# A graph attention layer on one core: SyncE fetches the rows of one gathered tile in every 22nd pair

## The chip, the cores and the metric

The kernel runs on one core of a Trainium2 chip. A core has five engines with a queue of instructions each: TensorE (PE), VectorE (DVE), ScalarE (ACT), GpSimd (POOL) and SyncE (SP). DMAs are issued from a queue of an engine and run on 16 DMA engines. The metric is the device time in microseconds, the median of the runs.

## The reference, cut to what matters

One layer of graph attention (GATv2) with layer norms and a feed forward part, on 12,500 nodes of 128 features and 400,000 edges. The edges are sorted by destination. All is in float32.

```python
h = relu(layernorm(x))
hn = ln1(h)
x_l, x_r = hn @ W_l, hn @ W_r                      # [nodes, 8 heads, 16]
m = leaky_relu(x_l[src] + x_r[dst] + ea @ W_e, 0.2)  # per edge
alpha = einsum("ehc,hc->eh", m, att)
a = softmax of alpha over the edges of one destination (and a self loop)
o = segment_sum(x_l[src] * a, dst) + bias
h = h + o
out = x + h + gelu(ln2(h) @ W1 + b1) @ W2 + b2
```

What matters here is `x_l[src]`: for each edge one row of 136 numbers (544 B: the 128 of x_l and eight ones for the sum of weights) is fetched from `xl_dram` by the index of the source. These are 3125 tiles of 128 edges.

## The kernel before, in words

**Units.** A unit is 256 edges (two tiles of 128), a pair is two units (512 edges, four tiles), and four pairs share one window of nodes. There are 782 pairs. The nodes are in 98 tiles of 128.

**The start.** A first stage reads x and writes the rows of x_l to `xl_dram` (`x_l`, L595 and L603, four tiles of nodes at a time). It also loads the edges' sources (`src_sb`, L797, one column per tile), the first destinations (`first_sb`, `base_sb`, L266) and makes the tables from which SyncE later reads addresses (`win_sb`, `base_sb`). Meanwhile GpSimd gathers raw rows of x for 29 pairs (`raw`, L301), stores them (`raw_dram`), and their x_l is worked out later from these (`late_dram`), so that these 29 pairs need no gather from `xl_dram`.

**The rounds.** The rest (`window_edges`) is one long list written out by hand, a loop over rounds `r`. Each engine has its instructions in the order of this list. In round `r` the steps of the list are applied to pair `c = r - late`, where `late` stands in a table:

- `gather` (-4): GpSimd issues four indirect DMAs, one for each tile of the pair, into `xs` (L980). Twelve buffers.
- `windows` (-3, once in four pairs): SyncE issues the loads of the edges' features `ea` (L994, two buffers, each freed by `combine` of its last pair), of the destinations `dl` and `du` (L999, L1004), reads one address from `win_sb` (L955) and loads the window of x_r, `zw` (L1010).
- `place` (-1): DVE makes the one-hot matrices. `combine` (0): PE transposes the rows of `xs` (L1034) and adds the window's product (L1037).
- `slope`, `bend`, `apart`, `score`, `lowest`, `weigh`, `turn`, `keep_turned` (1 to 5): the scores and their exponentials.
- `collect` (6): PE sums the weighted rows of `xs` (L1097). It is the last reader of `xs`.
- `own_heads` (7): DVE picks the heads and writes the records of the pair, `rec` (L1106, L1112).
- `put` (7): SyncE stores the record to `state` at an address read from `base_sb` (L1122, L955). Windows of 16 nodes of neighbouring units overlap, so stores are in order.

Between these stand the steps of node groups (four tiles of nodes, once all edges of the group are stored): loads of x_l, x_r and x, of the states (`f_state`, L1173), the end of the softmax and the feed forward part, and the store of the output (L1423). A group's round is found from the last unit that can touch its nodes (`done_after`). Further steps work out x_r (`xr_steps`) and the rows of the 29 late pairs (`raw_steps`), and in the first 196 rounds sum the edges' features (`ea_s`, L1129).

**Clearing.** `state` has two halves, for even and odd units. `clear` (L745) writes an empty value to seven tiles of nodes, a DMA for each half, once before the rounds and then every eighth round.

A DMA that touches bytes that an earlier one touches waits for it on the issuing engine: clearings, stores and the groups' loads of `state` have addresses from registers, so each is ordered behind the others.

Of the kernel before, what the change touches and what calls it, by code (L numbers as in the profile page):

```python
# [22 lines left out]
P = 128  # L23
H = 8
# [18 lines left out]
OW = 172  # L43
OS = 176
PW = OR * OS
BEFORE = 12
AFTER = 3
WN = P - DE
# [6 lines left out]
NQ = 16  # L55
SPARE = 8
AHEAD = 4
WAHEAD = 3
XR_STEPS = 6
RAW_MORE = 6  # L60
RAW_SHIFT = 8
# [1 line left out]
BUSY = 5  # L63
LEAD = 2
KEPT = 7
BIG = 2.0**126
CAP = 2.0**120

# [59 lines left out]
def raw_pairs(nt, n_edges):  # L128

    n_pr = -(-n_edges // (UP * U))  # L130
    at = [xr_round(t, nt, n_edges) + XR_STEPS + 1 for t in range(GN, nt, GN)]
    at = at[:-1] + [r + RAW_SHIFT for r in at[:RAW_MORE]]
    return [(r + RAW_STEPS + AHEAD + 1, r) for r in at if r + RAW_STEPS + AHEAD + 2 < n_pr]


def heads_of(nc, pool, out, att_c, fh):
# [8 lines left out]
def tile_gnn(  # L145
# [54 lines left out]

    h_sb = keep.tile([P, NT, P], F32, name="h_sb")
    src_sb = keep.tile([P, NCH * K], I32, name="src_sb")
    base_sb = keep.tile([1, NU // UP], I32, name="base_sb")
    win_sb = keep.tile([1, NU // QU], I32, name="win_sb")
# [49 lines left out]
    def load_consts():  # L254
        for i, v in enumerate((ln2_g, ln2_b, None, b1[0:P], b1[P : 2 * P])):
            if v is not None:
                nc.sync.dma_start(cols[:, 2 + i : 3 + i], column(v))
        nc.sync.dma_start(att_c, bass.AP(tensor=att.tensor, offset=att.offset, ap=[[1, C], [C, H], [1, 1]]))
        nc.sync.dma_start(we_sb, bass.AP(tensor=w_e.tensor, offset=w_e.offset, ap=[[P, DE], [0, QP], [1, P]]))
        nc.sync.dma_start(weh_sb[WN:P, :], w_e)  # L260
        nc.sync.dma_start(w1_sb, w1)
        nc.sync.dma_start(w2_sb, w2.rearrange("(k p) f -> p k f", p=P))
        nc.sync.dma_start(bias_r, row_bcast(bias, P))
        nc.sync.dma_start(b2_r, row_bcast(b2, P))
        for t, at in ((first_sb, 0), (base_sb, U)):
            nc.sync.dma_start(t, bass.AP(tensor=dst.tensor, offset=dst.offset + at, ap=[[0, 1], [UP * U, NU // UP]]))  # L266
# [103 lines left out]
    def edge_constants():  # L370
        of = build.tile([P, H], F32, name="of")
        mine = build.tile([P, H], F32, name="mine")
        below = build.tile([P, P // NW], F32, name="below")
        nc.vector.tensor_scalar(win_sb, first_sb[:, 0 : NU // UP : QP], float(P * 4), None, op0=OP.mult)
        nc.vector.tensor_scalar(first_sb, first_sb, float(BEFORE), None, op0=OP.add)
        nc.vector.tensor_tensor(base_sb, base_sb, first_sb, op=OP.min)
        nc.vector.tensor_scalar(base_sb, base_sb, float(H * SH * 4), None, op0=OP.mult)
# [362 lines left out]

    empty = keep.tile([P, H, SH], F32, name="empty")

    def clear(g):
        for st in state:
            nc.sync.dma_start(  # L745
                st.rearrange("(t p h) f -> p t (h f)", p=P, h=H)[:, g * GT : (g + 1) * GT, :],
                empty.rearrange("p h f -> p (h f)")[:, None, :].to_broadcast([P, GT, SW]),
            )

    node_stages = (  # L750
        (0, x_stats),
# [16 lines left out]
    with tc.manual_schedule():  # L768
# [15 lines left out]
        for r in range(max(max(len(qs), 9) + LAST + 1, 16 + PARTS, rows_at[-1] + KEPT + 1)):  # L784
# [10 lines left out]
                last_of_units()  # L795
            if r == 14:
                nc.sync.dma_start(src_sb, src)  # L797
            if r == 10:
                from_first()
            if 0 <= r - 10 < PARTS:  # L800
# [21 lines left out]
        clear(0)  # L822
    pre.close()

    fast = nc.values_load(flag[0:1, 0:1], min_val=0, max_val=1)
    with tc.If(fast == 1) as cmp:
        window_edges(
            tc, n_edges, ea_t, NT, NE, NUE, ident, wer, weh, negrep, diag, nid, farw, bias_r, b2_r, w1_sb, w2_sb,
            cols, xl_dram, xl_t, xr_dram, xr_t, dc_dram, du_dram, late_dram, state_dram, state, clear, xr_steps, qs, raw_steps, raw, x_t, out_t, h_sb, src_sb, base_sb, win_sb, wid,
        )  # L830
    with cmp.Else():
        any_edges(
# [64 lines left out]

def window_edges(
    tc, n_edges, ea_t, NT, NE, NUE, ident, wer, weh, negrep, diag, nid, farw, bias_r, b2_r, w1_sb, w2_sb,
    cols, xl_dram, xl_t, xr_dram, xr_t, dc_dram, du_dram, late_dram, state_dram, state, clear, xr_steps, qs, raw_steps, raw, x_t, out_t, h_sb, src_sb, base_sb, win_sb, wid,  # L900
):


# [25 lines left out]
    with ExitStack() as es:  # L929
# [34 lines left out]
        def states_at(at):  # L964
# [4 lines left out]
                "u (n f) -> n u f", f=SH * 4  # L969
            )  # L970

        def gather(c):
            xs = rows.tile([P, KP, XW], F32, name="xs")
            if c in of_raw:
# [2 lines left out]
                return  # L977
            for t in tiles_of(c):
                for j in t:
                    nc.gpsimd.indirect_dma_start(  # L980
                        out=xs[:, j, :],
                        out_offset=None,
                        in_=xl_dram,
                        in_offset=bass.IndirectOffsetOnAxis(ap=src_sb[:, c * KP + j : c * KP + j + 1], axis=0),
                    )
            pairs[c]["xs"] = xs

        def windows(c):
            if c % QP:
# [19 lines left out]
            at = words(win_sb[0:1, c // QP : c // QP + 1], NT * P * P * 4)[0]  # L1009
            nc.sync.dma_start(zw[0:WN, :].bitcast(U8), rows_at(xr_dram, at, WN, P * 4))  # L1010
# [18 lines left out]
        def combine(c):  # L1029
# [2 lines left out]
            z = ps2.tile([P, EPR], F32, name="z")  # L1032
            for j in range(e // P):
                nc.tensor.matmul(  # L1034
                    z[:, j * P : (j + 1) * P], d["xs"][:, j, 0:P], ident, start=(j == 0), stop=False, is_transpose=True
                )
            nc.tensor.matmul(z[:, :e], d["zw"], d["ea"][:, :e], start=False, stop=True)  # L1037
            d["z"] = z
# [51 lines left out]
        def collect(c):  # L1090
# [4 lines left out]
            for i, js in enumerate(tiles_of(c)):  # L1095
                for j in js:
                    nc.tensor.matmul(  # L1097
                        d["acc"][:, i, :], d["pt"][:, j * P : (j + 1) * P], d["xs"][:, j, :],
                        start=(j == js[0]), stop=(j == js[-1]),
                    )  # L1100

# [13 lines left out]

        def put(c):
            if c % QP == 0:
                at = words(base_sb[0:1, c : c + QP], NT * P * H * SH * 4)
                for i in range(c, min(c + QP, n_pr)):
                    pairs[i]["put"] = at[i - c]  # L1120
            d, nu = pairs[c], len(tiles_of(c))
            nc.sync.dma_start(states_at(d["put"])[:, 0:nu], d["rec"][:, 0:nu].bitcast(U8))  # L1122


        sums = [None] * NL
# [43 lines left out]
        def f_state(d):  # L1169
            n, ts = d["n"], d["ts"]  # L1170
            d["st"] = own_tile(d, "st", lambda n: [P, 2, n, SW], F32, "big", 3)
            for i in range(2):
                nc.sync.dma_start(d["st"][:, i, 0:n], state[i].rearrange("(t p h) f -> p t (h f)", p=P, h=H)[:, ts, :])  # L1173

        def f_load(d):
            n, ts = d["n"], d["ts"]
# [245 lines left out]
        def f_put(d):  # L1422
# [114 lines left out]
        last_round = n_pr + LATE + 2  # L1537
        free = SUM_STEP * (NL - 1) + 7
        for d, u in zip(groups, done_after(NT, n_edges)):
            d["round"] = max(free, (u // UP if u < NUE else n_pr) + LATE + 2)  # L1540
            free = d["round"] + GAP
        end["round"] = n_pr + LATE + 2

# [14 lines left out]
        CLEAR = 8  # L1558
        with tc.manual_schedule():
            for r in range(-AHEAD, max(last_round, groups[-1]["round"] + 18)):  # L1560
                in_round(r, early, groups[:-2])
# [15 lines left out]
                in_round(r, last_steps, groups[-1:])  # L1577
                in_round(r, enumerate(xr_steps), qs[1:])
                in_round(r, enumerate(raw_steps), raw)
                for late, f in late_stages:  # L1580
                    c = r - late
                    if 0 <= c < n_pr:
# [355 lines left out]
```

## Time and profile before

| | |
|---|---|
| median of 3 runs | 3962.19 us |
| the runs | 3970.01, 3962.19, 3960.23 us |
| the profiled execution | 3956.45 us |
| its span (first to last instruction) | 3954.7 us |
| busy share PE, DVE, ACT, POOL | 87%, 71%, 55%, 75% |
| granted TensorE clock, mean | 0.943 |
| DMA | 552.09 MB, mean 140 GB/s |

A group of instructions in the profile is a line of the program, an engine and an operation, what it writes and reads, the count, the busy time and the mean of one in ns, and behind the bar the idle time of the engine just before them with what ended it. "issue" is time in which the engine waited for nothing that the profile shows. SPq is SyncE's queue; its issuing instructions are not counted as busy, but each has a start and a length. Times of a timeline are start and length in us, from the start of the span.

### The profile page before, as it was taken

What the parts mean: (1) busy time and instruction counts of PE and PEld (TensorE: products, weight loads), DVE (VectorE), ACT (ScalarE), POOL (GpSimd) and SP (SyncE); (2) the same over time, 40 slices, a digit from 0 to 9 for tenths busy, and PEclk for the clock granted to TensorE, in tenths of its full rate; (3) what the DMA queues carried; (4) which work ended last, traced back from release to release, by engine and by line L of the source; (5) the groups of instructions that cost most, each with busy time, mean ns of one, the idle gap of its engine ahead of it and who ended that gap; (6) DMA issues with size and microseconds to landing.
All of it is one profiled execution on the core that took longest, in us unless ns stands there. A gap on an engine that the chain in (4) does not pass through costs nothing. (4 is left out here: it accounts for less than half of the span.)

```text
span 3954.7 us, 58500 instructions
## 1 busy us (share of the span) xinstructions
PE 3447.8 (87%) x18462; PEld 2358.8 (60%) x18463; DVE 2792.9 (71%) x6137; ACT 2168.7 (55%) x4747; POOL 2956.0 (75%) x3138
## 2 busy tenths in 40 slices
PE   4589898989898899999898898998889899889898
PEld 3356565656565666666665665666666566556565
DVE  6577777878776767677767776777767667667665
ACT  7445555655565555555555555555555555455444
POOL 7777777777777777777777777777777777777774
PEclk6799999999999999999999999999999999999999
DMA  8777787777666666666566666556556665655553
GB/s 225 214 183 190 195 201 194 184 176 168 164 128 124 128 122 123 128 123 120 115 122 128 124 123 128 123 119 125 117 124 125 127 122 108 122 119 114 122 118 74
DMA packets 579318, 552.09 MB, mean 140 GB/s; under 512 B 286689, under 2 KB 457282, under 8 KB 578578
## 3 DMA queue, kind: packets, MB, share of 16 engines
q1 hardware_dynamic: 478280, 330.80, 35.9%
q0 software_dynamic: 100000, 217.32, 28.5%
q8 instruction: 150, 2.46, 0.3%
q14 instruction: 168, 1.38, 0.1%
q10 hardware_dynamic: 720, 0.13, 0.0%
HBM read 482.05 MB, written 65.88 MB: 139 GB/s over the span
## 5 line engine op out<-in xcount | busy, mean ns | idle before, releaser
L980 POOL DMA_INDIRECT xs<-xl_dram,src_sb x3009 | 2841.7, 944 | 917.1 <-issue 798.0
L1075 ACT ACTIVATE p<-ab,rec 128x256 f32<-128x256 f32 x1563 | 655.2, 471 | 1025.8 <-DVE rec L1064 1021.3
L1106 DVE TENSOR_TENSOR own<-acc,diag 128x272 f32<-128x272 f32 x782 | 341.4, 437 | 811.5 <-PE acc L1097 809.5
L1097 PE MATMUL acc<-xs,pt 128*128 128x136 f32 x6250 | 891.6, 288 | 0.3 <-DVE own L1106 0.3
L1034 PE MATMUL z<-ident,xs 128*128 128x128 f32 x3125 | 552.9, 283 | 374.0 <-DMA xs<-xl_dram,src_sb 324.9
L1037 PE MATMUL z<-ea,zw 128*128 128x512 f32 x1564 | 852.7, 628 | 26.5 <-DVE ea L1020 11.3
L1034 PEld LDWEIGHTS z<-ident,xs 128*128 128x128 f32 x3125 | 398.4, 143 | 768.4 <-DMA xs<-xl_dram,src_sb 413.6
L1097 PEld LDWEIGHTS acc<-xs,pt 128*128 128x128 f32 x6250 | 820.7, 199 | 0.5 <-DVE own L1106 0.5
L1058 PE MATMUL ab<-m,negrep 128*128 128x512 f32 x1564 | 806.4, 597 | 0.0
L1088 ACT COPY pt<-pt_ps 128x512 f32<-128x512 f32 x782 | 454.9, 582 | 570.9 <-PE pt_ps L1083 568.9
L1053 DVE TENSOR_TENSOR m<-z,zs 128x512 f32<-128x512 f32 x782 | 532.8, 681 | 139.2 <-ACT zs L1048 138.1
L1083 PEld LDWEIGHTS pt_ps<-ident,p 128*128 128x128 f32 x3125 | 415.9, 148 | 360.1 <-issue 286.4
L1020 DVE TENSOR_SCALAR ea<-dl,wid 96x516 f32<-96x516 bf16 x782 | 575.8, 736 | 36.1 <-DMA dl<-dc_dram 36.1
L1064 DVE TENSOR_REDUCE rec<-ab 128x2 f32<-128x512 f32 x781 | 538.0, 689 | 13.1 <-PE ab L1058 12.5
L1083 PE MATMUL pt_ps<-ident,p 128*128 128x128 f32 x3125 | 499.4, 285 | 1.2 <-ACT xr L627 0.9
L1048 ACT ACTIVATE zs<-z 128x512 f32<-128x512 f32 x782 | 472.7, 604 | 41.7 <-DMA xs<-xl_dram,src_sb 34.9
L1112 DVE TENSOR_REDUCE rec<-own 128x34 f32<-128x272 f32 x782 | 340.8, 436 | 26.7
L1043 PE MATMUL ab<-ne,farw 128*128 128x512 bf16 x782 | 313.0, 400 | 28.4 <-ACT p L1075 25.7
L1037 PEld LDWEIGHTS z<-ea,zw 128*128 128x128 f32 x1564 | 256.5, 205 | 30.1 <-DVE ne L1027 10.3
L1058 PEld LDWEIGHTS ab<-m,negrep 128*128 128x128 f32 x1564 | 245.1, 194 | 1.1 <-DMA ea_s<-in_ea_t 0.7
L1043 PEld LDWEIGHTS <-farw 128*128 128x128 bf16 x782 | 79.5, 102 | 221.9 <-issue 110.2
L1075 ACT ACT_TABLE_LOAD x104 | 133.4, 1283 | 1.8
(237 smaller groups left out, 2167.4 us busy)
## 6 DMA issues: line engine op xcount, KB each, us to landing
dl<-dc_dram SPq DMA_DIRECT2D x196, 396.0 KB
ea<-in_ea_t SPq DMA_DIRECT2D x196, 256.0 KB
ea_s<-in_ea_t SPq DMA_DIRECT2D x98, 512.0 KB
xs<-xl_dram,src_sb POOLq DMA_INDIRECT x3009
state<-empty SPq DMA_DIRECT2D x28, 504.0 KB
state<-rec SPq DMA_DIRECT2D x781, 18.0 KB
f_st<-state SPq DMA_DIRECT2D x46, 288.0 KB
du<-du_dram SPq DMA_DIRECT2D x196, 64.0 KB
```

Source lines behind the costliest of these rows:

```text
L980: nc.gpsimd.indirect_dma_start(out=xs[:, j, :], out_offset=None, in_=xl_dram, in_offset=bass.IndirectOffsetOnAxis(ap=src_sb[:, c * KP + j ...
L1020: nc.vector.tensor_scalar(d["ea"][0:WN].rearrange("p (a b) -> p a b", b=OW), d["dl"][0:WN].rearrange("p (a b) -> p a b", b=OS)[:, :, 0:OW] ...
L1034: nc.tensor.matmul(z[:, j * P : (j + 1) * P], d["xs"][:, j, 0:P], ident, start=(j == 0), stop=False, is_transpose=True)
L1037: nc.tensor.matmul(z[:, :e], d["zw"], d["ea"][:, :e], start=False, stop=True)
L1048: nc.scalar.activation(d["zs"][:, :e], d["z"][:, :e], AF.Copy, scale=SLOPE)
L1053: nc.vector.tensor_tensor(d["m"][:, :e], d["z"][:, :e], d["zs"][:, :e], op=OP.max)
L1058: nc.tensor.matmul(d["ab"][:, :e], negrep.rearrange("p n h -> p (n h)"), d["m"][:, :e], start=False, stop=True)
L1064: nc.vector.tensor_reduce(d["rec"][:, :, CX], d["ab"].rearrange("p (u e) -> p u e", e=U), AX.X, OP.min)
L1075: nc.scalar.activation(d["p"][:, us], d["ab"][:, us], AF.Exp, bias=d["rec"][:, i, CX:SH], scale=-1.0)
L1083: nc.tensor.transpose(d["pt_ps"][:, js], d["p"][:, js], ident)
L1088: nc.scalar.copy(d["pt"][:, :e], d["pt_ps"][:, :e])
L1097: nc.tensor.matmul(d["acc"][:, i, :], d["pt"][:, j * P : (j + 1) * P], d["xs"][:, j, :], start=(j == js[0]), stop=(j == js[-1]),)
```

## The change

- Every 22nd pair from 30 to 778 (35 pairs, `hand_pairs`) gets only three gathers from GpSimd. The rows of its last tile are fetched by SyncE: 128 DMAs of one row each, at an address that SyncE reads from a table `hand_sb` (16 at a time), into one of two tiles of their own. They are spread over 22 rounds that end two rounds before the pair's use (`hand`). Each counts up one of seven semaphores, and SyncE waits for the full count in the round before the pair's use; PE's use is ordered behind this wait.
- `hand_sb` (35 partitions of 128 indices) is loaded at the start right behind `src_sb`, by one DMA of single words, and multiplied by the length of a row on DVE two rounds later.
- The addresses of windows and stores stand in one table `at_sb`, five words for four pairs, read at once. It is loaded by four DMAs in place of one.
- Loads of `windows` are issued four rounds ahead (`WAHEAD`, 3 before), and `put` stands one round later (`LATE + PUT`, 8 in place of 7). The node groups' rounds move with it, and `done_after` counts 12 nodes more.
- `clear` writes one tile of nodes for both halves in one DMA, four tiles before the rounds and then one every fourth round. A clearing isn't ordered behind stores so far, and a store isn't ordered behind loads of node groups before it. Stores stay ordered among themselves.

```diff
-WAHEAD = 3
+WAHEAD = 4
+PUT = 2
+BEHIND = 3
+HAND_EVERY = 22
+HAND_FIRST = 30
+HAND_LEAD = 2
+HAND_READ = 16
+LANDED = 7
...
-    return [-(-(t + n) * P * edges_per_node(nt, n_edges) // U) + SPARE for t, n in node_groups(nt)]
+    return [-(-((t + n) * P + BEFORE) * edges_per_node(nt, n_edges) // U) + SPARE for t, n in node_groups(nt)]
...
+        for i in range(QP):
+            nc.sync.dma_start(
+                at_sb[:, BEHIND:, 1 + i],
+                bass.AP(tensor=dst.tensor, offset=dst.offset + (UP * i + 1) * U, ap=[[0, 1], [QU * U, NQU]]),
+            )
...
             if r == 14:
                 nc.sync.dma_start(src_sb, src)
+                nc.sync.dma_start(
+                    hand_sb,
+                    bass.AP(
+                        tensor=src.tensor, offset=src.offset + (hands[0] + 1) * UP * KU - 1,
+                        ap=[[hands.step * UP * KU, len(hands)], [NCH * K, P]],
+                    ),
+                )
+            if r == 16:
+                nc.vector.tensor_scalar(hand_sb, hand_sb, float(XW * 4), None, op0=OP.mult)
...
+        def hand(r):
+
+            i, k = divmod(r + HAND_LEAD + hands.step - hands[0], hands.step)
+            if k == HAND_LEAD - 1 and 0 < i <= len(hands):
+                all_here = nc.sync.wait_ge(landed[(i - 1) % LANDED], ((i - 1) // LANDED + 1) * P * 16)
+                tc.declare_fence(all_here.ins, group=f"hand{i - 1}")
+            if not 0 <= i < len(hands):
+                return
+            d = by_hand[hands[i]]
+            if k == 0:
+                d["x"] = once.tile([P, XW], F32, name=f"hand{i % 2}")
+            for e in range(P * k // hands.step, P * (k + 1) // hands.step):
+                if e % HAND_READ == 0:
+                    d["at"] = words(hand_sb[i : i + 1, e : min(e + HAND_READ, P)], (NT * P - 1) * XW * 4)
+                row = nc.sync.dma_start(
+                    d["x"][e : e + 1, :].bitcast(U8), rows_at(xl_dram, d["at"][e % HAND_READ], 1, XW * 4)
+                )
+                row.then_inc(landed[i % LANDED], 16)
+                tc.no_tile_sem_insts.add(row.ins.name)
+                tc.add_to_no_dep_group(f"hand{i}", row.ins)
...
             for t in tiles_of(c):
                 for j in t:
+                    if c in by_hand and j == KP - 1:
+                        continue
                     nc.gpsimd.indirect_dma_start(
...
-            nc.sync.dma_start(states_at(d["put"])[:, 0:nu], d["rec"][:, 0:nu].bitcast(U8))
+            store = nc.sync.dma_start(states_at(d["put"])[:, 0:nu], d["rec"][:, 0:nu].bitcast(U8))
+            tc.add_to_no_dep_group("states", store.ins)
+            if c < n_pr - 3 * QP:
+                tc.declare_no_dep(
+                    store.ins, group="merged",
+                    reason="pairs behind a node group's round begin above its nodes, which the check of destinations asks",
+                )
...
-            (LATE + 1, put),
+            (LATE + PUT, put),
...
-                if r > 0 and r % CLEAR == 0 and r // CLEAR < NT // GT:
-                    clear(r // CLEAR)
...
+                hand(r)
+                t, off = divmod(r, CLEAR)
+                if off == 0 and CLEARED <= t + CLEARED < NT and t >= 0:
+                    tc.declare_no_dep(
+                        clear(t + CLEARED).ins, group="states",
+                        reason="states stored so far lie below the tile, which the check of destinations asks",
+                    )
```

More of the change, by code (lines that the diff above doesn't have):

```diff
@@ L133, in raw_pairs, with hand_pairs @@
     return [(r + RAW_STEPS + AHEAD + 1, r) for r in at if r + RAW_STEPS + AHEAD + 2 < n_pr]
+def hand_pairs(nt, n_edges):
+    late = {c for c, _ in raw_pairs(nt, n_edges)}
+    hands = range(HAND_FIRST, n_edges // (UP * U), HAND_EVERY)
+    assert not late & set(hands)
+    return hands
 def heads_of(nc, pool, out, att_c, fh):
@@ L821, in tile_gnn @@
                 first_xr[r - LAST](qs[0])
-        clear(0)
+        for t in range(CLEARED):
+            clear(t)
     pre.close()
@@ L828, in tile_gnn @@
             tc, n_edges, ea_t, NT, NE, NUE, ident, wer, weh, negrep, diag, nid, farw, bias_r, b2_r, w1_sb, w2_sb,
-            cols, xl_dram, xl_t, xr_dram, xr_t, dc_dram, du_dram, late_dram, state_dram, state, clear, xr_steps, qs, raw_steps, raw, x_t, out_t, h_sb, src_sb, base_sb, win_sb, wid,
+            cols, xl_dram, xl_t, xr_dram, xr_t, dc_dram, du_dram, late_dram, state_dram, state, clear, xr_steps, qs, raw_steps, raw, x_t, out_t, h_sb, src_sb, at_sb, hand_sb, hands, wid,
         )
@@ L899, in window_edges @@
     tc, n_edges, ea_t, NT, NE, NUE, ident, wer, weh, negrep, diag, nid, farw, bias_r, b2_r, w1_sb, w2_sb,
-    cols, xl_dram, xl_t, xr_dram, xr_t, dc_dram, du_dram, late_dram, state_dram, state, clear, xr_steps, qs, raw_steps, raw, x_t, out_t, h_sb, src_sb, base_sb, win_sb, wid,
+    cols, xl_dram, xl_t, xr_dram, xr_t, dc_dram, du_dram, late_dram, state_dram, state, clear, xr_steps, qs, raw_steps, raw, x_t, out_t, h_sb, src_sb, at_sb, hand_sb, hands, wid,
 ):
@@ L970, in states_at, with row_of @@
             )
+        by_hand = {c: {"i": i} for i, c in enumerate(hands)}
+        landed = [tc.alloc_semaphore(f"landed{i}") for i in range(LANDED)]
+        def hand(r):
[17 more added lines that the diff above has]
+                tc.add_to_no_dep_group(f"hand{i}", row.ins)
+        def row_of(c, j):
+            return by_hand[c]["x"] if c in by_hand and j == KP - 1 else pairs[c]["xs"][:, j, :]
         def gather(c):
@@ L986, in gather, with ats @@
             pairs[c]["xs"] = xs
+        read = {}
+        def ats(q):
+            if q not in read:
+                read[q] = list(words(at_sb[0:1, q], NT * P * H * SH * 4))
+                read[q][0] = nc.s_assert_within(
+                    read[q][0], 0, NT * P * P * 4, skip_runtime_bounds_check_because="the first node of four pairs is a node"
+                )
+            return read[q]
         def windows(c):
@@ L1539, in window_edges @@
         for d, u in zip(groups, done_after(NT, n_edges)):
-            d["round"] = max(free, (u // UP if u < NUE else n_pr) + LATE + 2)
+            d["round"] = max(free, (u // UP if u < NUE else n_pr) + LATE + PUT + 1)
             free = d["round"] + GAP
```

49 lines of the change are left out of this document (28 added, 21 removed).

## The prediction

> **What bounds the kernel now.** I read the page first, then GpSimd's waits, the gather line on its own, the chain, and last SyncE's waits and issue times.
>
> ```profile
> span 3954.7 us, 58500 instructions
> L980 POOL DMA_INDIRECT xs<-xl_dram,src_sb x3009 | 2841.7, 944 | 917.1 <-issue 798.0
> ```
>
> The page puts PE at the top by busy share, but the row to read is the gather's. 2841.7 us busy and 917.1 us idle make 3758.8 us, nearly the whole span. What is that idle time?
>
> ```profile
> POOL xs L980 <- issue: 798.0, 2618, 0.3
> POOL xs L980 <- DMA xs<-xl_dram,src_sb: 44.5, 146, 0.3
> L980 POOL DMA_INDIRECT xs<-xl_dram,src_sb x3009: 940/944/1080, 151.6 to 3909.2; - x189
> ```
>
> The columns of a wait are total, times, longest. No idle piece before a gather is longer than 0.3 us, whoever is named: 917.1 / 3009 = 0.305 us is a fixed gap, not a wait. So GpSimd never waits for data or for a buffer. The period is (3909.2 - 151.6) / 3008 = 1.249 us. The time is the start (151.6), 3009 periods, and a tail.
>
> ```profile
> 3907.92 3.38 DMA xs<-xl_dram,src_sb
> 3926.48 1.65 DMA state<-rec
> 3928.27 2.02 DMA state<-rec
> 3930.41 1.44 DMA state<-rec
> 3931.86 2.85 DMA f_st<-state
> ```
>
> These pieces of the chain (start, length, what) show the tail. The last gather lands, the last six rounds drain, three state stores follow one another, and the last node group is loaded and finished. The chain's printed shares hold this tail alone, so they don't name the bound. The gather row does.
>
> PE, next in line, is not near it. A pair has four gathers, 5.0 us, and this stretch of 3600 us has
>
> ```profile
> sum 3600.00, PE 3215.55 PEld 2192.68 DVE 2582.97 ACT 1977.56 POOL 2721.57; mean PE 357.28 PEld 243.63 DVE 287.00 ACT 219.73 POOL 302.40
> ```
>
> PE at 89%, and a 1% faster GpSimd asks 90% of it.
>
> **What SyncE does now.**
>
> ```profile
> SPq L1122 <- DMA state<-rec: 1359.2, 547, 8.2
> SPq L1122 <- DVE rec L1112: 739.1, 425, 8.9
> SPq L1122 <- DMA state<-empty: 85.8, 14, 9.3
> SPq L1122 <- DMA f_st<-state: 64.5, 24, 4.4
> ```
>
> More than half of SyncE's time is waiting at the state store, for the store before it, for this round's DVE, for clearings, and for a node group's load. None of it reaches GpSimd, which had no wait at all. That time is room for other work.
>
> **The change, part by part.**
>
> 1. Gathers removed. Pairs 30, 52, ... 778 lose the gather of their last tile: 35 pairs, 35 gathers. GpSimd's list is shorter by just these. 35 x 1.249 = 43.7 us come off a chain without slack. All lie before the last gather, so the tail follows GpSimd. This term has one answer as long as nothing else makes GpSimd wait.
>
> 2. Row fetches added. Each taken tile is fetched by SyncE as 128 DMAs of one row (544 B), spread over 22 rounds, 5.8 a round, with eight register loads of 16 addresses. Nothing of before is such a fetch. The nearest rows (the four-round loads and stores, the words they read, and early DMAs, of which L328, L337 and L421 go to one partition):
>
> ```profile
> L1010 SPq DMA_DIRECT2D zw<-xr_dram x196: 332/343/359, 159.6 to 3897.6; - x196
> L1010 SPq MOVE zw<-xr_dram x196: 29/35/42, 159.5 to 3897.5; - x196
> 27.89 0.22 SPq L328 DMA_DIRECT2D dc<-in_dst  x1
> 28.16 0.32 SPq L333 DMA_DIRECT2D dc<-in_dst  x1
> 28.52 0.27 SPq L337 DMA_DIRECT2D dc<-in_dst  x1
> 48.34 0.61 SPq L421 DMA_DIRECT2D lu<-in_dst  x1
> L955 SPq TENSOR_LOAD <-win_sb x196: 527/748/812, 158.7 to 3896.8; - x196
> L994 SPq DMA_DIRECT2D ea<-in_ea_t x196: 339/412/1699, 154.8 to 3894.3; - x196
> L999 SPq DMA_DIRECT2D dl<-dc_dram x196: 320/422/1731, 156.2 to 3894.7; - x196
> L1004 SPq DMA_DIRECT2D du<-du_dram x196: 584/593/1115, 157.5 to 3896.1; - x196
> L1122 SPq DMA_DIRECT2D state<-rec x782: 350/395/1278, 192.0 to 3930.4; - x196
> L1129 SPq DMA_DIRECT2D ea_s<-in_ea_t x98: 346/464/816, 160.1 to 1075.8; - x98
> L745 SPq DMA_DIRECT2D state<-empty x28: 377/488/687, 153.4 to 665.0; - x28
> ```
>
> With a move of 0.035 and some 0.05 between instructions (28.52 - 27.89 less 0.22 and the 0.32 of the one between leaves 0.09 for two gaps), a row costs from 0.22 + 0.085 = 0.30 us to 0.61 + 0.085 = 0.70. zw, the one fetch at an address from a register, gives 0.43. One partition costs less than 96 in two of three rows, so I take 0.42. Then 22 rounds cost 128 x 0.42 + 8 x 0.75 = 60 us of SyncE.
>
> Its other work in 22 rounds: 22 stores at 0.395, 5.5 times ea, dl, du, zw and one register load (0.412 + 0.422 + 0.593 + 0.343 + 0.748 = 2.52), some eight DMAs of node groups and late pairs at 0.4, and 0.05 or a move for each: 8.7 + 13.9 + 3.2 + 4 = 30 us. In the first 196 rounds eleven ea_s (5.1), and in the first 376 clearings (2.7), make 38. GpSimd's 22 rounds last 22 / 781 x 2974 x 1.249 = 104.6 us. SyncE is taken for 90 of 104.6, early 98. It keeps up, and the rows cost nothing on GpSimd's chain. This is the cover of the whole gain: it fails at a row price of (104.6 - 30 - 6) / 128 = 0.54 us (early 0.47).
>
> 3. The wait for the rows. SyncE waits in the round before the pair's use, two rounds after the last row was issued. Behind it in the queue stand the loads four rounds ahead and the stores, and PE waits for it at this pair's first transposes. Landings take 3.38 us for a gather and 1.4 to 2.0 for a store. Two rounds are 9.5 us. So nothing. If it is late, PE stops, but GpSimd not at once. It has 12 buffers of a pair, and each is freed by the product six rounds behind the transposes, so PE, which now runs right behind the gathers, can fall some five pairs (24 us) back first.
>
> 4. Stores a round later, clearings and stores free of each other, loads four rounds ahead. These remove waits of SyncE (85.8 and 64.5, and part of 739.1). GpSimd gains nothing from that. Consecutive stores are still ordered: in the order of instructions each names the DMA of the one before, so the 1359.2 shrinks only because rows fill the time. ea's load now comes one round after its buffer is freed and will wait for PE, with rows queued behind it. That holds SyncE to PE's pace, not below it. Cost 0, both ways.
>
> 5. The start. A gather table of 35 x 128 single words (hand_sb) is loaded right behind src_sb, and DVE multiplies it two rounds later, ahead of everything else in its queue. Four address loads in place of one come earlier, each like first_sb's (0.61 us of SyncE), near 44 us.
>
> ```profile
> 1.28 3.10 SPq L283 DMA_DIRECT2D src_raw<-in_src  x2
> 43.91 0.61 SPq L266 DMA_DIRECT2D first_sb<-in_dst  x1
> 8.71 0.95 POOL L301 DMA_INDIRECT raw<-in_x,src_raw  x1 [0.30 <-issue]
> 71.97 0.70 SPq L797 DMA_DIRECT2D src_sb<-in_src  x1
> 60.00:80.00 20.00, 8.93 (x36) 7.34 (x36) 18.83 (x97) 17.26 (x71) 15.49 (x15) 0.50 0.64 196
> 77.81 0.42 DVE L439 CAST df<-dc 98x512 f32<-98x512 int32 x1
> 136.65 0.37 SPq L603 DMA_DIRECT2D xl_dram<-xl  x1
> 151.60 0.94 POOL L980 DMA_INDIRECT xs<-xl_dram,src_sb  x1 [0.30 <-issue]
> ```
>
> The CAST at 77.81 is the instruction that the multiplication precedes. src_sb's 1.6 MB at 196 GB/s (last column) is there at about 81. src_raw, 3712 short runs, was issued at 1.28 and there by 8.4, so 4480 words take at most 8.6 us: about 89.5. DVE would stand 12 us. What does that reach? The last x_l store is issued at 136.65 and, landing in 3.4, is there at 140.4. The first gather that needs it starts at 151.60. So 11 us are free for this and for the 1.8 us of the address loads, and I put the cost at 1 us, with ends 0 and 11.5 (below).
>
> By the Trainium skill (DMA: Bandwidth & Descriptors, section on why a DMA increments its semaphore by 16) a DMA runs on the largest number of engines up to 16 that divides its slowest dimension. For 35 partitions that is 7, where src_raw's 128 give 16. No row shows the engines of one DMA. This rule speaks against the change, and by it the sum would lose the 11.5 us of the rival on the start.
>
> 6. The tail. The last but one node group moves two rounds back, so its last step falls into the drain:
>
> ```profile
> 3913.22 0.68 DVE L1314 TENSOR_TENSOR f_x<-f_x,h_sb 128x512 f32<-128x512 f32 x1
> ```
>
> At most 0.68 beside PE's drain: 0.5. If the last stores did overlap, up to 3.5 of the chain's 5.1 us of stores would go. I take none.
>
> Sum: -43.7 + 0 + 0 + 0 + 1 + 0.5 = -42.2 us. The profiled execution took 3956.45 us (span 3954.7), which gives 3914.3. The three runs had a median of 3962.19, 5.7 above it, so I forecast 3962.2 - 42.2 = 3920.
>
> **Rivals.**
>
> SyncE becomes the bound (slower). From a row price of 0.54 us on, 22 rounds last as long as SyncE's list, and GpSimd stops once its buffers are full. Each 0.01 us above adds 35 x 1.28 = 45 us. At 0.60, 22 rounds are 112.8 against 105.9 before (3009 gathers), so 35 x 6.9 + 9 x 8 for the early ones = 314 us: 4276. For it: the 0.61 row. Against: the other two and zw. 9%.
>
> The start costs the slack. If the words of hand_sb come at 7/16 of src_raw's rate, they take 19.6 us, DVE stands until 100.5, 22.7 us, and 11.5 are left over after the slack. Then -43.7 + 11.5 + 0.5 = -31.7: 3930. For it: short runs on fewer partitions. Against: 8.6 is itself an upper bound. 14%.
>
> The rows come late often. SyncE reaches some waits behind PE, GpSimd stops at times, and half the gain goes: 3941. Early rounds with 98 of 104.6 are where. 6%.
>
> The change doesn't do what it says: GpSimd's period grows with SyncE's added DMAs, by 0.014 us, and eats the gain: 3962. Against: the 944 ns median lies at the minimum, 940, at every load of the DMA engines. 2%.
>
> **How the numbers follow.** The forecast has 69%, the rivals 9, 14, 6 and 2. The range runs from the fastest run, 3960.2 - 43.7 - 3.5 with 3 us of spread, 3910, to the half-lost gain, 3943. It leaves out SyncE as the bound. About 0.3%, 12 us, is what a measurement of this kernel can tell from no change. Faster by more: 69 + 14 + 4 of the 6 = 87%; within: 4%; slower: 9%.
>
> **What would show it.** Right: 2974 gathers at a 1.249 us period with idle pieces of 0.3 us, and a last gather that starts near 3867. Row fetches of 0.3 to 0.5 us, and stores that no longer wait over 1000 us. A DVE wait of some 10 us for hand_sb near 78, with the first gather from xl_dram still near 152. Wrong: gathers that wait for PE's product (L1097), SyncE without idle time and rows over 0.54 us, or a first gather after 156.

## The result: no gain, 1.0017 of the time before

| kernel | median | runs | profiled span |
|---|---|---|---|
| before | 3961.83 us | 20 (3958.22 to 3970.01) | 3954.7 us |
| after | 3968.51 us | 20 (3961.08 to 3977.47) | 3963.6 us |

The ratio of the runs is 1.0017, with a 95% interval of 1.001 to 1.0024. The forecast was 3920. So some 50 us of gain are missing, and the profile says where they went. The page of the profile of after first: span, the gather's group (busy, mean ns, idle and what ended most of it), and the chain by engine.

```profile
span 3963.6 us, 67630 instructions
L1046 POOL DMA_INDIRECT xs<-xl_dram,src_sb x2974 | 2809.1, 945 | 956.1 <-issue 767.4
PE 42%; DMA 22%; POOL 12%; issue 9%; DVE 8%; SPq 4%; ACT 3%; POOLq 0%; DVEq 0%; ACTq 0%
```

The 35 gathers are gone, and one gather still takes 945 ns. But the idle time in front of them grew: 2974 fixed gaps of 0.305 us would make 907 us, and there are 956, so 49 us are new. The chain, which held only the tail before, now runs through PE, DMA and SyncE. The waits of after (total us, times, longest us) name the new idle pieces:

```profile
POOL xs L1046 <- issue: 767.4, 2516, 0.6
POOL xs L1046 <- PE acc L1173: 72.1, 89, 5.7
POOL xs L1046 <- PE z L1110: 19.2, 50, 4.3
DVE part L1216 <- DMA ea_s<-in_ea_t: 81.2, 36, 3.9
DVE ea L1096 <- DMA dl<-dc_dram: 59.7, 32, 6.3
PE z L1110 <- SPq L1015: 78.7, 16, 8.0
```

A gather now stands up to 5.7 us until the product at L1173 frees a row buffer. DVE waits for the loads of the sums (ea_s) and of the windows (dl), and PE for SyncE's wait at L1015, that for the rows.

Where in time is this? The busy-time view by stretches (length, then busy us of PE, PEld, DVE, ACT, POOL, the granted clock, DMA share, GB/s), first two rows of before, then the same two of after:

```profile
450.00:1250.00 800.00, 711.42 (x3838) 484.29 (x3839) 615.12 (x1225) 440.09 (x957) 604.91 (x641) 0.96 0.74 171
1300.00:3100.00 1800.00, 1625.48 (x8816) 1113.74 (x8815) 1276.13 (x2705) 1010.24 (x2062) 1360.77 (x1442) 0.96 0.61 123
```

```profile
450.00:1250.00 800.00, 682.82 (x3626) 463.26 (x3625) 580.42 (x1160) 415.29 (x915) 567.67 (x602) 0.94 0.73 163
1300.00:3100.00 1800.00, 1635.49 (x8977) 1123.73 (x8976) 1299.63 (x2754) 1025.03 (x2101) 1360.48 (x1441) 0.97 0.63 128
```

From 1300 us on GpSimd is as busy as before, 1360.48 against 1360.77: no stall, and the later hand tiles pay in full. All of the loss lies in 450 to 1250 us: (604.91 - 567.67) / 604.91 x 800 = 49 us. That is the part in which SyncE also loads ea_s for the sums. The sums alone don't make the loss: rows and sums both run from 200 to 450 us too, and there GpSimd is busy for 189.00 us, before the change for 188.78. The chain from 500 to 1200 us, by line and by some of its longest pieces (start, length, what):

```profile
by line: DMA dl<-dc_dram 10.6%; DMA ea_s<-in_ea_t 8.6%; PE z L1113 8.4%; PE acc L1173 7.6%; PE ab L1134 6.4%; issue 6.4%; PE pt_ps L1159 4.1%; DMA xr<-raw_dram 4.0%; DMA du<-du_dram 3.9%; PE z L1110 3.8%; SPq L1025 3.2%; DVE part L1216 3.1%
619.60 7.13 DMA dl<-dc_dram
660.71 6.53 DMA dl<-dc_dram
679.41 7.05 DMA dl<-dc_dram
```

The largest items on the chain are loads that SyncE issues, and the gather is not among them. SyncE's own waits in 450 to 1050 us, the three largest of before, then of after, and last from the DMA view the stores that after issued there, one a round:

```profile
SPq L1122 <- DMA state<-rec: 235.3, 105, 5.2
SPq L1122 <- DVE rec L1112: 78.8, 49, 4.4
SPq L1122 <- DMA state<-empty: 40.2, 6, 8.0
```

```profile
SPq L1197 <- DMA state<-rec: 54.8, 40, 2.8
SPq L1197 <- DMA state<-empty: 11.3, 12, 1.7
SPq L1197 <- DVE rec L1188: 5.2, 16, 0.5
```

```profile
state<-rec SPq DMA_DIRECT2D x119, 18.0 KB
```

All rows of the waits together make 385.7 us of 600 before and 89.7 after. SyncE went from waiting 64% of the time to 15%. In after, its work is (600 - 89.7) / 119 = 4.29 us a round, and a round takes 600 / 119 = 5.04. Late, from 1300 to 3100, it waits 258.2 of 1800 us (14%) over 381 rounds: 4.05 us of work in rounds of 4.72.

The rows themselves are cheap. The issue lines of after (min/median/max ns), and a stretch of SyncE in order of time, where the gaps between DMAs are inside the groups:

```profile
L1025 SPq DMA_DIRECT2D hand<-xl_dram x4480: 224/228/535, 183.8 to 3891.8; - x195
L1025 SPq MOVE hand<-xl_dram x4480: 29/29/38, 183.8 to 3891.8; - x195
L991 SPq TENSOR_LOAD <-hand_sb x280: 979/1264/2013, 182.7 to 3881.5; - x140
L991 SPq TENSOR_LOAD <-at_sb x199: 546/1586/1666, 159.4 to 3935.3; - x199
```

```profile
2004.01 0.42 SPq L1197 DMA_DIRECT2D state<-rec  x1
2004.53 1.88 SPq L1025 DMA_DIRECT2D hand<-xl_dram  x6
2006.57 0.42 SPq L1197 DMA_DIRECT2D state<-rec  x1
```

Six rows take 1.88 us, so 0.32 us each with move and gaps.

### The profile page after: what moved, and what is told of

Read it like the earlier page. It is cut to its first block, busy times and chain, and to the rows that moved or that the text cites. A ratio compares the mean times of both kernels' runs of the same rounds, so it can differ in the third digit from the quotient of the medians.

```text
span 3963.6 us, 67630 instructions
## 1 busy us (share of the span) xinstructions
PE 3427.3 (86%) x18461; PEld 2345.1 (59%) x18463; DVE 2795.3 (71%) x6140; ACT 2160.9 (55%) x4745; POOL 2923.6 (74%) x3103
## 4 chain that ended last, share of the span: by engine, by line
PE 42%; DMA 22%; POOL 12%; issue 9%; DVE 8%; SPq 4%; ACT 3%; POOLq 0%; DVEq 0%; ACTq 0%
DMA xs<-xl_dram,src_sb 12%; POOL xs L1046 12%; PE z L1113 10%; PE acc L1173 9%; PE ab L1134 8%; PE pt_ps L1159 5%; PE z L1110 5%; DMA dl<-dc_dram 3%; PE ab L1119 2%; DMA ea_s<-in_ea_t 2%; DVE rec L1140 1%; SPq L1025 1%; DMA xr<-raw_dram 1%; DVE ea L1096 1%; SPq L991 1%
## 5 line engine op out<-in xcount | busy, mean ns | idle before, releaser
L1046 POOL DMA_INDIRECT xs<-xl_dram,src_sb x2974 | 2809.1, 945 | 956.1 <-issue 767.4
L1173 PE MATMUL acc<-xs,pt 128*128 128x136 f32 x6180 | 877.4, 286 | 2.3 <-DVE f_wt L1327 2.3
L1173 PEld LDWEIGHTS acc<-xs,pt 128*128 128x128 f32 x6180 | 805.6, 198 | 2.8 <-issue 1.6
L1110 PE MATMUL z<-ident,xs 128*128 128x128 f32 x3090 | 532.1, 282 | 286.6 <-DMA xs<-xl_dram,src_sb 213.9
L1119 PE MATMUL ab<-ne,farw 128*128 128x512 bf16 (+1 forms) x781 | 308.9, 396 | 36.9 <-ACT p L1151 36.9
L1216 DVE TENSOR_REDUCE part<-ea_s 128x1 f32<-128x1024 f32 x98 | 118.7, 1211 | 81.7 <-DMA ea_s<-in_ea_t 81.2
```

The costliest lines, as they stand in the source:

```text
L1046: nc.gpsimd.indirect_dma_start(out=xs[:, j, :], out_offset=None, in_=xl_dram, in_offset=bass.IndirectOffsetOnAxis(ap=src_sb[:, c * KP + j ...
L1110: nc.tensor.matmul(z[:, j * P : (j + 1) * P], row_of(c, j)[:, 0:P], ident, start=(j == 0), stop=False, is_transpose=True)
L1119: nc.tensor.matmul(d["ab"][:, :e], d["far"], d["ne"][:, :e], start=True, stop=False)
L1173: nc.tensor.matmul(d["acc"][:, i, :], d["pt"][:, j * P : (j + 1) * P], row_of(c, j), start=(j == js[0]), stop=(j == js[-1]),)
```

## The experiments

After the result and the first runs there were these theories of the 49 us:

- A: the wait for the rows stands at the wrong place in SyncE's queue, one round before use.
- B: SyncE's queue is full in the early part.
- C: the transfers of the early part land later.
- D: the other parts of the change (stores, clearings, loads ahead) cost it.
- F: not SyncE's work but its waits for DVE hold the queue.
- G: each early hand tile costs some 5 us at PE, whatever SyncE's load.
- H: the stall belongs to the early part as such (the sums).

In e3, e2, every_18 and every_20 below, a wait that is always met (`nc.sync.wait_ge(started, 16)`) stands in place of the rows where a round has none to fetch.

**Without hand tiles (e3_no_hand).**

```diff
-        by_hand = {c: {"i": i} for i, c in enumerate(hands)}
+        by_hand = {}
...
         def hand(r):
+            nc.sync.wait_ge(started, 16)
+            return
```

> The whole change without any hand tile: all tiles are gathered by GpSimd, no row is fetched by SyncE (a wait that is always met keeps the place of the rows in its queue). Stores a round later, clearings, loads four rounds ahead and the words of four pairs at once stay. Theories A, B and C: as before, 3958 to 3966. Theory D: slower than before by the stall of the early part, 3990 to 4015.

Measured: 3960.82 us against 3960.99, ratio 1.0001 (0.9992 to 1.001). The stores, clearings and earlier loads by themselves cost nothing and bring nothing. D falls. SyncE waits 365.6 of 600 us here, at 129 rounds: 1.82 us of work a round. So the rows with their register loads are 4.29 - 1.82 = 2.47 us a round.

**Hand tiles only after the sums (e2_hand_late).**

```diff
-HAND_FIRST = 30
+HAND_FIRST = 228
```

> The whole change, but the first hand tile is that of pair 228 instead of pair 30, behind the last load for the sums: 26 tiles by hand instead of 35 (a wait that is always met keeps the place of the rows in SyncE's queue). Theories A, B and C: no stall of GpSimd before 1250 us, and 26 x 1.249 = 32.5 us less than before, 3928 to 3935. Theory D (it is the other parts, the stores a round later, the clearings by twos of tiles, the loads four rounds ahead, that hold up the early part, and not the hand rows): the stall of 450 to 1250 us stays, 3965 to 3980.

Measured: 3930.93 us, ratio 0.9922 (0.9909 to 0.9935). That is 30.1 us less than before, where 26 gathers are worth 32.5. The nine early tiles of the change don't bring 11 us: with them the kernel takes 38 us longer than without. GpSimd's row of the early part is that of before again (604.94):

```profile
450.00:1250.00 800.00, 719.71 (x3839) 489.46 (x3838) 614.55 (x1217) 439.24 (x950) 604.94 (x641) 0.95 0.78 171
```

Late, SyncE waits here 270.0 of 1800 us, 15%, as in after, and nothing stalls.

**The rows and the wait for them three rounds earlier (e1_fence_early).**

```diff
-HAND_LEAD = 2
+HAND_LEAD = 5
...
-            if k == HAND_LEAD - 1 and 0 < i <= len(hands):
+            if k == 1 and 0 < i <= len(hands):
```

> The whole change, but each hand tile's fetches start and its wait on SyncE stands three rounds earlier (the wait four rounds ahead of the pair instead of one). Theory A (the wait for the rows stands too late in SyncE's in-order queue: behind a store that waits for DVE and a window load that waits for PE, so PE gets the hand tile 4 to 8 us late, falls back, keeps the buffers of the rows, and GpSimd stalls): PE no longer waits at the hand pairs, GpSimd's idle time before its gathers falls by most of the 48 us, time 3920 to 3935. Theory B (SyncE simply has too much to issue while the loads for the sums run, the first 200 rounds): SyncE's work is the same, only moved by 3 rounds, and the loads of windows still come late; time 3955 to 3970. Theory C (the memory: the transfers of the early part, ea_s among them, take longer and the window loads land late): 3955 to 3970.

Measured: 3964.94 us, ratio 1.0007 (0.9999 to 1.0016). PE no longer waits for SyncE at any hand pair: that row is gone from the waits. The stall stays. Its early waits, and its busy row:

```profile
DVE part L1216 <- DMA ea_s<-in_ea_t: 90.9, 38, 3.7
POOL xs L1046 <- PE acc L1173: 49.3, 24, 7.2
DVE ea L1096 <- DMA dl<-dc_dram: 41.7, 26, 3.4
```

```profile
450.00:1250.00 800.00, 681.55 (x3623) 460.33 (x3624) 582.41 (x1162) 413.71 (x916) 569.98 (x604) 0.95 0.73 163
```

What comes late is now dl and ea_s, which stand in the same queue. A falls: the stall is there without PE's wait at the hand pairs.

**The loads for the sums on ScalarE's queue (e4_sums_act).**

```diff
-            nc.sync.dma_start(
+            nc.scalar.dma_start(
                 sums[i],
```

> The whole change, with the 98 loads for the sums issued from ScalarE's queue instead of SyncE's (the same transfers, 35 hand tiles). Theory B: SyncE is relieved of some 0.5 us every second round of the early part, the stall goes, 3918 to 3930. Theory A: the wait for the rows still stands behind the store and the window load, most of the stall stays, 3950 to 3968. Theory C: the transfers are the same and collide the same way, 3955 to 3970.

Measured: 3979.57 us, ratio 1.005 (1.0037 to 1.0063): slower than any of the three theories expected. SyncE's work fell to (600 - 112.4) / 120 = 4.06 us a round, as B wants, but SyncE got new waits, for transfers that ScalarE now issues:

```profile
SPq L1197 <- DMA state<-rec: 61.5, 48, 4.1
SPq L1197 <- DMA ea_s<-in_ea_t: 11.8, 3, 5.5
...
SPq L1039 <- DMA ea_s<-in_ea_t: 6.6, 1, 6.6
...
SPq L1081 <- DMA ea_s<-in_ea_t: 2.6, 1, 2.6
```

The relief, some 0.23 x 120 = 28 us, is nearly given back by these 21. That leaves no gain, but it does not say why the run is 11 us slower than after; this stays open. So the run neither confirms B nor removes it. In 450 to 1250 us DVE waits 75.0 us for dl and PE 50.4 for SyncE at the hand pairs, while 19% of SyncE's time are waits.

**Half the rate in the early part (g5_half_early).** Early hand tiles at pairs 30, 74, 118, 162 and 206, the rows of the last four spread over 44 rounds:

```diff
+        by_hand = {c: {"i": i} for i, c in enumerate(hands) if i % 2 == 0 or i > 8}
+        SLOW = hands[2:9:2]
...
+                n = 2 * hands.step if c in SLOW else hands.step
...
+            for e in range(P * k // n, P * (k + 1) // n):
```

> 31 tiles by hand: while the loads for the sums run half as often and their rows at half the rate, then every 22nd pair. Where the kernel before takes its usual time (near 3961): theory B (SyncE full in the early part, 98 of 100 us asked): early demand falls to 45 + 27 = 72 of 100, no stall, gain 31 x 1.249 = 38.7 us, 3919 to 3929. Theory G (each early hand tile costs some 5 us of its own at PE, whatever SyncE's load): 3940 to 3950. Where the kernel before takes some 4720 to 4770, as in the two runs of this kernel so far: slower than before by 2 to 4%.

Measured: 3924.13 us against 3958.8, ratio 0.9910 (0.9895 to 0.9926): 34.7 us less, where 31 gathers are worth 38.7. No stall is left on GpSimd, by the gather's group and by the busy row:

```profile
L1053 POOL DMA_INDIRECT xs<-xl_dram,src_sb x2978 | 2820.0, 947 | 908.5 <-issue 778.6 <-DMA xs<-xl_dram,src_sb 53.4 <-PE acc L1180 23.2
```

```profile
450.00:1250.00 800.00, 717.55 (x3862) 483.91 (x3862) 618.75 (x1231) 441.39 (x954) 605.09 (x639) 0.96 0.73 171
```

908.5 / 2978 is the fixed gap of 0.305 us again. SyncE waits 202.1 of the 600 us, 34%. Five early hand tiles that cost 5 us each would have cost 25. G falls: it is the rate. This is the fastest kernel here, beating both before and after.

**All rows fetched, none read (g7_rows_unused).**

```diff
-            return by_hand[c]["x"] if c in by_hand and j == KP - 1 else pairs[c]["xs"][:, j, :]
+            return pairs[c]["xs"][:, j, :]
...
-                    if c in by_hand and j == KP - 1:
-                        continue
```

> All 4480 rows fetched and awaited by SyncE, read by nothing; GpSimd gathers all tiles as before. Where the kernel before takes its usual time: theory B: the early part runs at SyncE's pace of some 5.05 us a round against 4.81, 3990 to 4015. Theory G (the loss is PE's wait for the rows at the hand pairs): nobody waits for the rows, 3958 to 3967. Where the kernel before takes some 4720 to 4770: slower than before by 4 to 5.5%.

Measured: 3979.21 us against 3958.8, ratio 1.0052 (1.0038 to 1.0065). No engine but SyncE waits for these rows, and they still cost 20.4 us, less than B's 30 but not G's 0. SyncE waits 76.8 of the 600 us (13%), with the same 4.29 us of work over 122 rounds, and the early stall is there, smaller (waits of the whole run, then the busy row):

```profile
DVE part L1214 <- DMA ea_s<-in_ea_t: 71.8, 34, 4.6
POOL xs L1044 <- PE acc L1171: 38.6, 87, 4.3
```

```profile
450.00:1250.00 800.00, 703.46 (x3752) 478.31 (x3752) 593.03 (x1176) 422.94 (x933) 595.58 (x631) 0.95 0.71 168
```

**Other rates and a later store.** Three more kernels ran only on other chips of the kind, three of them, on which the kernel before itself took 4720 to 4770 us; half_early and rows_unused had also run on one of these, twice. The ratios are to before on the same chip.

Expected of half_early there, first and second run:

> The whole change, but while the loads for the sums run the hand tiles come half as often and their rows at half the rate: pairs 30, 74, 118, 162, 206, each of the last four spread over 44 rounds, then every 22nd pair as before; 31 tiles by hand. Theory B (SyncE is full in the early part: it waits 55 us of 100 there without rows, late 64, and rows at this rate take about 53 of 100, so 98 are asked early and 89 late): early demand falls to 45 + 27 = 72 of 100, no stall, gain 31 x 1.249 = 38.7 us, 3919 to 3929. Theory G (each early hand tile costs some 5 us of its own, by its wait at PE, whatever SyncE's load): 5 of 9 such costs stay, 3940 to 3950.

> The same kernel as half_early once more, on a chip on which the kernel before takes its usual time (31 tiles by hand: in the early part half as often and at half the rate of rows). Theory B (SyncE full in the early part, 98 of 100 us asked): early demand falls to 45 + 27 = 72 of 100, no stall, gain 31 x 1.249 = 38.7 us, 3919 to 3929. Theory G (each early hand tile costs some 5 us of its own at PE, whatever SyncE's load): 3940 to 3950.

Of every_18 (`HAND_FIRST = 228`, `HAND_EVERY = 18`), three runs:

> The hand tiles start at pair 228 as in the run without early tiles, but come every 18th pair instead of every 22nd: 31 tiles. Theory B (SyncE full): late demand rises from 36 + 53 = 89 to 36 + 65 = 101 of 100 us, so the stall that after had early now comes late, over some 2700 us: slower than before, 3980 to 4150. Theory H (the stall belongs to the early part itself: DVE with the sums, the transfers of the sums): no stall late, gain 31 x 1.249 = 38.7, 3920 to 3930.

> The same kernel as every_18 once more (31 tiles by hand, from pair 228 on, every 18th pair). Theory B: late demand on SyncE rises from 36 + 53 = 89 to 36 + 65 = 101 of 100 us, the stall comes late, slower than before, 3980 to 4150. Theory H (the stall belongs to the early part itself: DVE with the sums, the transfers of the sums): gain 31 x 1.249 = 38.7, 3920 to 3930.

> 31 tiles by hand, from pair 228 on, every 18th pair. Where the kernel before takes its usual time: theory B: SyncE is asked for 36 + 65 = 101 of 100 us late, so the stall of the early part comes late, over some 2700 us: slower than before, 3980 to 4150. Theory H (the stall belongs to the early part itself: DVE with the sums, the transfers of the sums): no stall late, gain 31 x 1.249 = 38.7, 3918 to 3930. Where the kernel before takes some 4720 to 4770: slower than before by 7 to 8%, as in its two runs there.

Of rows_unused, two runs:

> SyncE fetches and awaits all 4480 rows as in the whole change, but nothing reads them: GpSimd gathers all tiles as before the change, and PE and the products read the gathered tiles. Theory B (SyncE full early): the early part runs at SyncE's pace of some 5.05 us a round against 4.81, +30 to +50 us, 3990 to 4015. Theory G (the loss is PE's wait for the hand rows at the hand pairs): nobody waits for the rows, as before, 3958 to 3967.

> The same kernel as rows_unused once more (all 4480 rows fetched and awaited by SyncE, read by nothing; GpSimd gathers all tiles). Theory B: the early part runs at SyncE's pace of some 5.05 us a round against 4.81, 3990 to 4015. Theory G (the loss is PE's wait for the rows at the hand pairs): nobody waits for the rows, 3958 to 3967.

Of put_later (`PUT = 3`), four runs:

> The whole change with the stores one round later still (PUT 3 instead of 2). SyncE's work is the same; its queue then waits less for DVE's results, on which it spends 6 to 10 us of 100 in the early part. Theory B (SyncE has too much of its own to issue early): 3958 to 3972. Theory F (the queue has room, but loses it in waits for DVE's results in front of the stores): those waits go, most of the 48 us stall goes, 3922 to 3940.

> The same kernel as put_later once more (the whole change, stores one round later still). Theory B: SyncE's own work is the same, 3958 to 3972. Theory F (SyncE's queue has room, but loses it in waits for DVE's results in front of the stores): 3922 to 3940.

> The whole change with the stores one round later still (PUT 3). Where the kernel before takes its usual time: theory B (SyncE has too much of its own to issue early): 3958 to 3972. Theory F (the queue has room, but loses it in waits for DVE's results in front of the stores, 6 to 10 us of 100 early): 3922 to 3940. Where the kernel before takes some 4720 to 4770: slower than before by 4 to 5.5%.

> The whole change with the stores one round later still (PUT 3). Where the kernel before takes its usual time: theory B (SyncE has too much of its own to issue early): 3958 to 3972. Theory F (the queue has room, but loses it in waits for DVE's results in front of the stores, 6 to 10 us of 100 early): 3922 to 3940. Where the kernel before takes some 4720 to 4770: slower than before by 4 to 5.5%.

Of every_20 (half_early with `HAND_EVERY = 20`):

> Hand tiles every 20th pair, and in the early part every 40th with the rows spread over 40 rounds: 34 tiles by hand (a wait that is always met keeps the place of the rows where none is due). Theory B: SyncE is asked for 45 + 29 = 74 of 100 us early and for 36 + 58 = 94 late, under 100 but over the 89 that went without a stall: without a stall 34 x 1.249 = 42.5 us less, 3916 to 3924; if its limit is near the 94, slower than half_early, 3925 to 3960.

Measured:

| kernel | ratio there |
|---|---|
| half_early | 1.0369, 1.0235 |
| rows_unused | 1.0536, 1.0448 |
| put_later | 1.0551, 1.043, 1.0522, 1.0512 |
| every_20 | 1.0587 |
| every_18 | 1.08, 1.071, 1.0795 |

There the time rises with the rate of rows, and rows_unused takes as long as put_later, which reads its rows and gathers 35 tiles fewer. But even half_early loses there, so these runs don't decide the case of the usual chip. For every_18, every_20 and put_later (theories F and H) it stays open. F has the trace of after against it: from 450 to 1050 us SyncE waits for DVE 18.2 of 600 us, which is 3 of 100 and not the 6 to 10 expected, and in no_hand, which does not stall, it is 27.9.

What is settled: the loss comes from hand tiles in the early part (e2, e3), through the rate of their rows (g5), and partly through fetching them alone (g7). It is not the place of the wait (e1), and not a tile's own cost (g5). C has the trace against it, though no run tested it alone: the early DMA share is 0.73 in after and 0.74 before, and by the semaphore records of the traces a dl load of 650 to 1050 us took at the median 6.5 us from issue to landing in after, 6.7 in before and 7.9 without rows. The loads were late because they were issued late, and the instruction starts show it. From the issue of a dl load to its first use by DVE, at the median of the loads of 650 to 850 us, it is 7.0 us in after and 6.4 in rows_unused, hardly more than the landing, but 12.2 in no_hand and 13.7 in half_early. In after it was still 14.0 from 200 to 450 us, and it is 13.3 again from 1700 us on. (Such a short time alone does not stop GpSimd: before, which issues these loads a round later, had 7.7 from 450 to 650 us.)

What stays open is the split. Rows that nobody reads cost 20 us, while the change is 49 short. The rest should come from the ring in which PE waits for SyncE's loads, DVE for PE, and SyncE's next store for DVE, but that is argued, not shown.

## Why the prediction was wrong, step by step

1. Gathers removed, -43.7: right in kind and price. 2974 gathers of 945 ns, and late, where nothing stalls, they pay: after gives back there what it lost early.

2. Row fetches, cost 0: this step failed, in "It keeps up, and the rows cost nothing on GpSimd's chain". They cost 49 us. The sum in front of it was good. I put SyncE's list at 98 us for 22 early rounds and 90 for late ones. Measured: 22 x 4.29 = 94 and 22 x 4.05 = 89. The row was cheaper (0.32 instead of 0.42), and the register loads were dearer (1.26 instead of 0.75, and 1.59 for the five words of four pairs). Most of these errors cancelled, which was luck.

What was wrong is the criterion. I compared the work with the period and called 94% of it enough. But SyncE works in order and has waits of its own in between, for the landing of the store before (2.8 us at the median there, not the 1.4 to 2.0 that I read from the tail) and for DVE's results. In the early stretch, with GpSimd stalled, 15% of the time were still such waits: its work filled 85%, not 100%. Nor is the early period 104.6 us: without rows an early round takes 600 / 129 = 4.65 us, so 22 take 102 (8 of these 129 rounds belong to late pairs, which need no gather, against 12 of 373 from 1300 to 3100 us). Asked were 94 of 102, 92%. Late it was 89 of 104 (22 x 4.72), 86%, and that went without a stall; by the rounds without rows there, 1800 / 373 = 4.83, it is 84%. From 200 to 450 us, where SyncE waits 41.7 us, it was (250 - 41.7) / 49 = 4.25 us a round of 250 / 51 = 4.90 without rows, 87%, without a stall too.

No share is a limit by itself, though: with the loads on ScalarE's queue (e4) 4.06 of 4.65 was 87% as well, and it stalled, with more waits in the queue. That there is an edge between 87 and 92% is inferred from these stretches; every_18 on the usual chip would have tested it late.

3. The wait for the rows, cost 0: half failed. PE waits at the hand pairs up to 8.0 us. Late its buffers absorb that, as the step said. Early they don't, and e1 shows that the stall stays even without this wait.

4. Stores, clearings, earlier loads, 0: right, 1.0001 without the rows.

5. The start, 1 us: right in its cost, 0.6. DVE stood for hand_sb 8.9 us (12 expected), and the first gather from xl_dram starts at 152.2, against 151.6. The pieces were off both ways: by the semaphore records src_sb was there at 86.4 us, not near 81, and hand_sb 4.3 us behind it, not 8.6.

```profile
DVE hand_sb L832 <- DMA hand_sb<-in_src: 8.9, 1, 8.9
```

```profile
L1046 POOL DMA_INDIRECT xs<-xl_dram,src_sb x2974: 938/944/1347, 152.2 to 3916.1; - x199
```

By the Trainium skill's rule on engines (DMA: Bandwidth & Descriptors, on why a DMA increments its semaphore by 16) this load runs on 7 engines. The trace agrees: the load's semaphore moves once 0.5 us after the issue and then seven times, from 12.3 to 13.7 us after it, while that of src_sb moves sixteen times. The 11.5 us that the rival on the start made of it did not come: 0.6 were lost.

6. The tail, 0.5: too small. From the start of the last gather to the end it is 3963.6 - 3916.1 = 47.5 us, against 45.5 before, so 2.0.

The row of gathers under step 5 gives the miss: the last gather starts at 3916.1, not near 3867. These 49 us are the stall of step 2, and the sign of being wrong that came is the one named first, gathers that wait for PE's product. Of the rivals, "the rows come late often" named the place and the mechanism, early rounds with 98 of 104.6, but put its loss at half of the gain and its chance at 6%. The loss was more than the whole gain. "SyncE becomes the bound" had the right engine and the wrong point: it asked a row price over 0.54 us (early 0.47), and the price was 0.32.

## What to carry to other kernels

A queue that works in order and also waits can be full before its work reaches the period: here 84 to 87% went in two stretches, 92% did not, and 87% with added waits did not either. So budget its work against the part of its time that it doesn't spend waiting, stage by stage, with the stage's own period. When work is moved to an idle engine, give each stage a rate that it can take. Five hand tiles in place of nine in the busy stage, with rows at half the rate, turned no gain into 0.9910.

## What was not expected of the hardware

Reading five words into registers took SyncE longer (1586 ns at the median) than reading sixteen (1264).

On the chips on which the kernel before took 4720 to 4770 us, SyncE's instructions themselves came late. In the last run of put_later there, the same move and the same row fetch have the medians of after, but maxima of 1.4 us, against 0.038 and 0.535 in after:

```profile
L1025 SPq MOVE hand<-xl_dram x4480: 1/29/1409, 257.4 to 4956.2; - x195
L1025 SPq DMA_DIRECT2D hand<-xl_dram x4480: 2/228/1437, 259.5 to 4957.6; - x195
```

From the start of one row fetch to that of the next it was 0.59 us at the median there, and 0.33 in after. So a kernel with 4480 more DMAs on one queue lost more there than its issue durations say. Why these chips are slower was not looked for.
